# Which PSUM banks the layernorms of a selective-scan stage use, in a kernel that overlaps the scan with the layers behind it

## Chip, cores, metric

The kernel runs on one core of a Trainium2 chip. The metric is device time in microseconds of one execution; lower is better. Times are medians of a few runs.

## What is computed

Input is x, 4 batches of 384 channels by 32 x 32 positions, all float32. Two layers, each a mixer and a feed-forward with residuals:

```
x = x + SS2D(ln_c(x))          # layer 0 mixer: 4-direction selective scan, layernorm, gelu
t = t + MoE(ln_t(t))           # layer 0 FFN: 4 experts, top 2, 384 -> 1536 -> 384
x = x + attention(ln_c(x))     # layer 1 mixer: 8 heads of 64, one weight for q, k and v
t = t + kron_mlp(ln_t(t))      # layer 1 FFN with Kronecker-factored weights

# the recurrence inside SS2D, for each direction k, channel d and state n, along 1024 positions
h = h * exp(dt * A) + dt * u * B
y = sum over n of h * C   (+ D * u)
ln(v) = (v - mean(v)) / sqrt(var(v) + eps)    # over the 384 channels
```

## The kernel before, in words

**The scan part** (`scan_layer`) walks over 32 units: 4 batches, 4 directions, 2 halves of 512 positions. Units 0 to 7 are batch 0, 8 to 15 batch 1, and so on. A unit has three chunks of 128 channels, a chunk four groups g of states (`chunk`, from line 388). Per chunk and group GpSimd multiplies dt*u by B (L419, two instructions of 128x1024), ScalarE makes exp(dt*A) into PSUM (L428), VectorE runs the recurrence (L433), VectorE and GpSimd multiply by C (L440, L447), and TensorE sums over the states into one PSUM bank `acc` with a selection matrix (L454). VectorE then adds `acc` into y (L281, L285). So a unit has 24 instructions of L419, and counting them tells where the scan stands. While a unit is scanned, `project` prepares the next one: matmuls for B, C and dt (L317, L344), the softplus on ScalarE (L348 to L361; for batches 1 to 3 GpSimd helps with L374 and L375), and stores to DRAM from which the scan's operands are read back broadcast by SyncE's DMA queue (L329, L403).

**The layernorms of the scan part** (`layernorm`, L155): over one half of 512 positions a ones-matrix matmul of three channel chunks gives the mean in one PSUM bank (L162), VectorE subtracts it (L164), ScalarE squares (L171), three more matmuls give the variance in a second bank (L175), ScalarE makes the inverse root (L148, L149), VectorE multiplies (L178). It is called for each batch's input (`start`: both halves, when the first unit of that batch is about to be prepared) and for each batch's output (`finish`: once for each half, after the last direction), 16 halves in all. `finish` continues with a GELU (L226), the residual add on GpSimd (L233) and the store to `x1`.

**The tail** (`tail_batch`) is everything after the scan for a batch: `route` (token transposes L635, router, placing of tokens by an indirect DMA L662), `experts` (11 slots: 8 of 256 rows and 3 of 128, each with its expert's two weight matrices fetched by SyncE: matmuls L906 and L921, transposes L889), `combine` (indirect gathers L951, matmuls L958), `prologue`, `attention` (L1007, scores L1030, weights times values L1076, division L1052) and `last_layers` (L1123, L1161, L1178, L1192). It is called from `between(b)`, which after batch b's scan calls the tail of batch b-1. The tail of batch 3 is called after the scan, with other pools.

**PSUM.** There are eight banks of 128 x 512 float32. In the scan part two hold `da` (pool `s_da`), two (pool `s_ps`, tag "ps") are shared by `acc`, the projections `xd_ps` and `dt_ps`, and the layernorms' `mean` and `var`; one (tag "o") and three (tag "p") belong to the `Room` of the tail. Nearly every matmul group of the tail takes a bank of tag "p" by `room.bank("p", ...)`.

**What sets the order.** A scheduler orders each engine's instructions when the program is built. It goes by priorities that follow the order in the source, with an estimate of durations, fills gaps with later work that is ready, and gives out the buffers of a pool by tag. Parts of the tail are marked with `high_priority(offset=FORWARD)`. What it has put in an engine's queue is then fixed. Source order at a batch's end is: `finish` of both halves of batch b, then `tail_batch(b-1)`, then the units of batch b+1.

Of the kernel before, what the change touches and what calls it, by code (L numbers as in the profile page):

```python
# [9 lines left out]
F32 = mybir.dt.float32  # L10
# [7 lines left out]
P = 128  # L18
# [5 lines left out]
HF = 512  # L24
NH = L // HF
# [87 lines left out]
class Body:  # L113
# [38 lines left out]
        at = COL[name][0] + i  # L152
        return self.cols[:, at : at + 1]

    def layernorm(self, src, dst, eps, psum, work, parts=range(NH)):  # L155

        nc = self.nc
        for i in parts:
            sl = halves(i)
            mean = psum.tile([P, HF], F32, tag="ps", name="ln_mean")  # L160
            for c in range(DC):
                nc.tensor.matmul(mean, self.ones, src[:, c, sl], start=(c == 0), stop=(c == DC - 1))  # L162
            for c in range(DC):
                nc.vector.scalar_tensor_tensor(  # L164
                    dst[:, c, sl], mean, -1.0 / D, src[:, c, sl], op0=ALU.mult, op1=ALU.add
                )

            sqs = []
            for c in range(DC):
                sq = work.tile([P, HF], F32, tag="k2", name="ln_sq", bufs=6)  # L170
                nc.scalar.activation(sq, dst[:, c, sl], AF.Square)  # L171
                sqs.append(sq)
            var = psum.tile([P, HF], F32, tag="ps", name="ln_var")
            for c in range(DC):
                nc.tensor.matmul(var, self.ones, sqs[c], start=(c == 0), stop=(c == DC - 1))  # L175
            self.inverse_root(var, var, eps, scale=1.0 / D)
            for c in range(DC):
                nc.vector.tensor_mul(dst[:, c, sl], dst[:, c, sl], var)  # L178

    def scan_layer(self, x1, between):

        nc, tc, a = self.nc, self.tc, self.a
        with ExitStack() as ctx:
            wp = ctx.enter_context(tc.tile_pool(name="s_w", bufs=1))
            work = ctx.enter_context(tc.tile_pool(name="s_work", bufs=1))
            dram = ctx.enter_context(tc.tile_pool(name="s_dram", bufs=3, space=DRAM))
            dap = ctx.enter_context(tc.tile_pool(name="s_da", bufs=2, space=PSUM))
            psum = ctx.enter_context(tc.tile_pool(name="s_ps", bufs=2, space=PSUM))  # L190

            wx = wp.tile([P, DC, KG, XD], F32, tag="wx", name="wx")
            nc.scalar.dma_start(out=wx, in_=a["wx"].rearrange("(c p) k m -> p c k m", p=P))
            nega = wp.tile([P, KG * NB * NG], F32, tag="nega", name="nega")
            lo, hi = COL["alog"]
            nc.scalar.activation(nega, self.cols[:, lo:hi], AF.Exp)
            nc.vector.tensor_scalar_mul(nega, nega, -1.0)
            dsum = wp.tile([P, DC], F32, tag="dsum", name="dsum")
            lo, hi = COL["ds"]
            nc.vector.tensor_reduce(  # L200
                dsum, self.cols[:, lo:hi].rearrange("p (k c) -> p c k", k=KG), AX.X, ALU.add
            )

            sel = wp.tile([P, DB], F32, tag="sel", name="sel")
            nc.vector.tensor_reduce(
                sel, self.ident.rearrange("p (n d) -> p d n", d=DB), AX.X, ALU.add
            )

            def start(b):
                x = work.tile([P, DC, L], F32, tag="u", name="u")  # L210
                src = a["x"][b].rearrange("(c p) l -> p c l", p=P)
                if b > 0:
                    nc.sync.dma_start(out=x, in_=src)
                    self.layernorm(x, x, self.eps6, psum, work)
                    return x

                for i in range(NH):
                    nc.sync.dma_start(out=x[:, :, halves(i)], in_=src[:, :, halves(i)])
                self.layernorm(x, x, self.eps6, psum, work, parts=[0])
                return x  # L220

            def finish(b, y, i):

                self.layernorm(y, y, self.eps5, psum, work, parts=[i])
                for c in range(DC):
                    ins = nc.scalar.activation(  # L226
                        y[:, c, halves(i)], y[:, c, halves(i)], AF.Gelu,
                        bias=self.col("lnb", c), scale=self.col("lnw", c),
                    ).ins
                    rows = slice(c * P, (c + 1) * P)  # L230
                    x = work.tile([P, HF], F32, tag="k2", name="x", bufs=6)
                    nc.sync.dma_start(out=x, in_=a["x"][b][rows, halves(i)])
                    nc.gpsimd.tensor_add(x, x, y[:, c, halves(i)])  # L233
                    nc.sync.dma_start(out=x1[b][rows, halves(i)], in_=x)
                self.exp_again(ins)

            units = [
                (b, k, i)  # L240
                for b in range(B)
                for k in ORDER
                for i in (range(NH) if k < 2 else reversed(range(NH)))
            ]
            us = {0: start(0)}
            ahead = []
            self.place_behind = None
            for _ in self.project(units[0], us[0], wx, work, dram, psum, ahead):
                pass
            self.layernorm(us[0], us[0], self.eps6, psum, work, parts=range(1, NH))  # L250
            self.under_way = {}
            carry = None
            for n, unit in enumerate(units):
                b, k, i = unit
                fed, ahead = ahead, []
                project = iter(())
                if n + 1 < len(units):
                    nb = units[n + 1][0]
                    if nb not in us:
                        us[nb] = start(nb)  # L260
                    project = self.project(units[n + 1], us[nb], wx, work, dram, psum, ahead)
                    next(project)
                if n % NH == 0:
                    carry = wp.tile([P, NB * NG], F32, tag=f"carry{n // NH % 2}", name="carry")
                if k == 0 and i == 0:
                    y = work.tile([P, DC, L], F32, tag="y", name="y")
                for c in range(DC):
                    acc = psum.tile([P, HF], F32, tag="ps", name="acc")
                    for _ in self.chunk(
                        unit, n % NH == 0, c, fed, carry, nega, sel, acc, work, dap  # L270
                    ):
                        next(project, None)
                    if k % 2 == 0:
                        ys = y[:, c, halves(i)]
                        out = acc
                    else:
                        w = slice(i * (HW // NH), (i + 1) * (HW // NH))
                        ys = y[:, c, :].rearrange("p (h w) -> p h w", h=HW)[:, :, w]
                        out = acc.rearrange("p (w h) -> p h w", h=HW)
                    if k == 0:  # L280
                        nc.vector.scalar_tensor_tensor(  # L281
                            ys, us[b][:, c, halves(i)], dsum[:, c : c + 1], out, op0=ALU.mult, op1=ALU.add
                        )
                    else:
                        nc.vector.tensor_add(ys, ys, out)  # L285
                if k == ORDER[-1]:
                    self.under_way.setdefault(b, fed[2])
                    finish(b, y, i)
                    if n + 1 == len(units) or units[n + 1][0] != b:
                        between(b)  # L290
# [1036 lines left out]
def build(nc, a):  # L1327
    with tile.TileContext(nc, schedule_with_timeline_sim=True) as tc, ExitStack() as ctx:
        body = Body(ctx, tc, a)
        dram = ctx.enter_context(tc.tile_pool(name="x1", bufs=1, space=DRAM))  # L1330
        x1 = [dram.tile([D, L], F32, tag=f"x1_{b}", name=f"x1_{b}") for b in range(B)]
        with ExitStack() as tail:
            room = body.open_tail(tail)

            def between(b):
                if b > 0:
                    body.tail_batch(b - 1, x1, room)

            with ExitStack() as banks:
                room.open_banks(banks, NARROW_BANKS)  # L1340
                body.scan_layer(x1, between)
                wide = Room(tc, tail, "w", WIDE)
                wide.open_banks(banks, NARROW_BANKS)
                body.route(B - 1, x1, wide)
                xc = body.first_layer(B - 1, wide)
            with ExitStack() as banks:
                wide.open_banks(banks, WIDE_BANKS)
                body.second_layer(B - 1, xc, wide, lambda: None)
                flag = body.overflow(wide)
# [79 lines left out]
```

## Time and profile before

| | |
|---|---|
| time, median of 3 runs | 4389.3 us (4378.26 to 4389.32) |
| the profiled execution, its own time | 4365.25 us |
| its span, first to last instruction | 4363.5 us |
| PE busy | 3382.3 us, 78% |
| POOL busy | 3049.6 us, 70% |
| DVE busy | 2919.3 us, 67% |
| ACT busy | 2504.0 us, 57% |
| mean granted TensorE clock | 0.86 |
| DMA moved | 684.74 MB, mean 157 GB/s |

Engines: PE is TensorE (PEld its weight loads), DVE VectorE, ACT ScalarE, POOL GpSimd, SP SyncE. In lines by 40 slices each digit is the busy share of one slice (109 us) in tenths. In lines of stretches the columns are start:end, length, then busy time (and instructions) of PE, PEld, DVE, ACT and POOL, the granted TensorE clock, DMA share and GB/s. A line of a group has: source line, engine, operation, written<-read tiles, shapes, count | busy us, mean ns | idle before it and what ended it. The trace counts each float32 matmul of this kernel as two.

### The profile page before, as it was taken

What the parts mean: (1) busy time and instruction counts of PE and PEld (TensorE: products, weight loads), DVE (VectorE), ACT (ScalarE), POOL (GpSimd) and SP (SyncE); (2) the same over time, 40 slices, a digit from 0 to 9 for tenths busy, and PEclk for the clock granted to TensorE, in tenths of its full rate; (3) what the DMA queues carried; (4) which work ended last, traced back from release to release, by engine and by line L of the source; (5) the groups of instructions that cost most, each with busy time, mean ns of one, the idle gap of its engine ahead of it and who ended that gap; (6) DMA issues with size and microseconds to landing.
All of it is one profiled execution on the core that took longest, in us unless ns stands there. A gap on an engine that the chain in (4) does not pass through costs nothing. (4 is left out here: it accounts for less than half of the span.)

```text
span 4363.5 us, 46084 instructions
## 1 busy us (share of the span) xinstructions
PE 3382.3 (78%) x13436; PEld 1581.3 (36%) x13436; DVE 2919.3 (67%) x4331; ACT 2504.0 (57%) x4470; POOL 3049.6 (70%) x1475
## 2 busy tenths in 40 slices
PE   6545544379997895579997888579998799999896
PEld 2111111145553221235554322135554234666323
DVE  5888888967877868968787867968887740200102
ACT  4445545556665875466575777466666564343353
POOL 5999998898988968688898978789898831000100
PEclk7766776589997997779998999679999899999997
DMA  5444354577886534457779534457789434336200
GB/s 136 114 122 116 106 162 115 151 228 214 231 241 183 142 109 139 125 174 213 213 229 279 154 95 132 115 158 225 215 233 273 134 108 142 116 126 214 63 17 15
DMA packets 404756, 684.74 MB, mean 157 GB/s; under 512 B 50960, under 2 KB 206480, under 8 KB 404496
## 3 DMA queue, kind: packets, MB, share of 16 engines
q1 hardware_dynamic: 395184, 655.37, 51.9%
q0 software_dynamic: 8192, 25.17, 1.7%
q8 instruction: 108, 1.77, 0.2%
q14 instruction: 152, 1.25, 0.1%
q10 hardware_dynamic: 1120, 1.18, 0.1%
HBM read 561.47 MB, written 120.06 MB: 156 GB/s over the span
## 5 line engine op out<-in xcount | busy, mean ns | idle before, releaser
L419 POOL TENSOR_TENSOR bx<-dtr,bcs 128x1024 f32<-128x1024 f32 x768 | 1792.4, 2361 | 229.6 <-PE acc L454 118.7
L428 ACT ACTIVATE da<-dtr,nega 128x512 f32<-128x512 f32 x1536 | 1045.3, 690 | 945.8 <-DVE bx L440 564.3
L447 POOL TENSOR_TENSOR bx<-bx,bcs 128x1024 f32<-128x1024 f32 x384 | 903.1, 2359 | 179.1 <-DVE carry L444 74.3
L906 PE MATMUL h_ps<-xc,w 128*128 128x256 f32 (+1 forms) x3168 | 675.0, 368 | 60.8 <-DMA w<-in_w 18.7
L454 PE MATMUL acc<-bx,sel 128*32 128x512 f32 x3072 | 496.8, 697 | 289.2 <-POOL bx L447 232.4
L921 PE MATMUL y_ps<-w,hs 128*128 128x384 f32 x1824 | 643.2, 505 | 38.1 <-ACT hs L914 37.8
L906 PEld LDWEIGHTS h_ps<-xc,w 128*128 128x128 f32 x3168 | 556.1, 200 | 238.7 <-issue 112.8
L433 DVE TENSOR_TENSOR_SCAN bx<-da,carry,bx 128x512 f32<-128x512 f32 x384 | 474.7, 1270 | 129.3 <-ACT da L428 65.8
L433 DVE TENSOR_TENSOR_SCAN bx<-da,bx 128x512 f32<-128x512 f32 x384 | 453.3, 1210 | 117.1 <-POOL bx L419 59.2
L433 DVE TENSOR_TENSOR_SCAN da<-da,carry,bx 128x512 f32<-128x512 f32 x384 | 478.0, 1274 | 66.5 <-ACT da L428 60.9
L440 DVE TENSOR_TENSOR bx<-da,bcs 128x512 f32<-128x512 f32 x768 | 510.3, 680 | 3.7
L433 DVE TENSOR_TENSOR_SCAN da<-da,bx 128x512 f32<-128x512 f32 x384 | 456.2, 1219 | 63.3 <-ACT da L428 53.0
L921 PEld LDWEIGHTS y_ps<-w,hs 128*128 128x128 f32 x1824 | 350.0, 196 | 325.8 <-issue 78.2
L1036 ACT ACTIVATE ex<-s_ps 128x512 f32<-128x512 f32 x512 | 300.8, 592 | 156.6 <-PE s_ps L1030 154.4
L1030 PE MATMUL s_ps<-w 64*128 64x512 f32 x1024 | 307.9, 662 | 53.1 <-ACT ex L1036 51.8
L911 ACT ACTIVATE hs<-h_ps,bb 128x256 f32<-128x256 f32 (+1 forms) x528 | 201.0, 441 | 218.8 <-PE h_ps L906 218.4
L1076 PE MATMUL o_acc<-ex,vt 128*64 128x512 f32 x1024 | 287.0, 638 | 18.1 <-ACT ex L1036 11.5
L454 PEld LDWEIGHTS acc<-bx,sel 128*32 128x32 f32 x3072 | 80.0, 116 | 585.9 <-POOL bx L447 319.8
L942 POOL TENSOR_TENSOR diag<-ident,g_weight 128x1024 f32<-128x1024 f32 x8 | 15.0, 1893 | 345.6 <-PE xc_ps L889 331.0
L925 DVE TENSOR_TENSOR y<-y_ps,bb 128x384 f32<-128x384 f32 x76 | 41.7, 549 | 273.4 <-PE y_ps L921 273.4
L344 PE MATMUL dt_ps<-xd,wdt 12*128 12x512 f32 x192 | 123.2, 726 | 71.4 <-ACT mag L383 43.8
L1030 PEld LDWEIGHTS s_ps<-w 64*128 64x128 f32 x1024 | 82.8, 190 | 256.0 <-ACT ex L1036 206.0
(214 smaller groups left out, 3767.2 us busy)
## 6 DMA issues: line engine op xcount, KB each, us to landing
w<-in_w SPq DMA_DIRECT2D x352, 576.0 KB
dtr<-dd SPq DMA_DIRECT2D x1536, 128.0 KB
bcs<-rows SPq DMA_DIRECT2D x512, 128.0 KB
dd<-one_e SPq DMA_DIRECT2D x96, 256.0 KB
dd<-mag SPq DMA_DIRECT2D x96, 256.0 KB
rows<-zero SPq DMA_DIRECT2D x76, 192.0 KB
xs<-rows SPq DMA_DIRECT2D x32, 384.0 KB
made<-y SPq DMA_DIRECT2D x32, 384.0 KB
```

What stands on the lines that cost most here:

```text
L419: pool = nc.gpsimd.tensor_mul(bx, dtr[q][1], bc[:, 0].unsqueeze(1).to_broadcast([P, 2, HF])).ins
L428: nc.scalar.activation(da, dtr[q][0][:, j, :], AF.Exp, scale=nega[:, col : col + 1])
L433: nc.vector.tensor_tensor_scan(run(h), run(da), run(bx[:, j, :]), 0.0 if first else hold, ALU.mult, ALU.add,)
L440: dve = nc.vector.tensor_mul(bx[:, j, :], h, cg).ins
L447: pool = nc.gpsimd.tensor_mul(bx, bx, cg.unsqueeze(1).to_broadcast([P, 2, HF])).ins
L454: nc.tensor.matmul(acc[lo : lo + DB, :], sel, out[q][:, j, :], start=(g == 0), stop=(g == NG - 1),)
L906: nc.tensor.matmul(ps[:, r, :], w1[(f + r) // wf][:, c, (f + r) % wf * P : ((f + r) % wf + 1) * P], xc[:, c, :], start=(c == 0), stop=(c = ...
L911: nc.scalar.activation(hs[:, f + r, :], ps[:, r, :], AF.Identity, bias=bb[:, f + r : f + r + 1])
L921: nc.tensor.matmul(out[:, :D], hs[:, f, t * P : (t + 1) * P], w2[f // wf][:, f % wf, :], start=(f == 0), stop=(f == FC - 1),)
L1030: ins = nc.tensor.matmul(ps, w[rows, j * P : (j + 1) * P], w[rows, halves(i)], start=True, stop=True).ins
L1036: done.append(nc.scalar.activation(ex[:, o, :], ps, AF.Exp, scale=HD**-0.5, accum_out=sums[:, t, 2 * j + o, i : i + 1],).ins)
L1076: ins = nc.tensor.matmul(out[cols, :], made[t][1][:, j, cols], ex[:, o, :], start=(j == 0), stop=(j == MB - 1),).ins
```

## The change

The layernorms of the scan part take their two banks (`ln_mean`, `ln_var`) from the tail's room, tag "p" (three banks), in place of the scan's own pool (tag "ps", two banks). The pools keep their sizes; the scan's two banks are now shared by `acc`, `xd_ps` and `dt_ps` alone. The `room` is handed through to `scan_layer`.

```
-    def layernorm(self, src, dst, eps, psum, work, parts=range(NH)):
+    def layernorm(self, src, dst, eps, room, work, parts=range(NH)):
...
-            mean = psum.tile([P, HF], F32, tag="ps", name="ln_mean")
+            mean = room.bank("p", "ln_mean")
...
-            var = psum.tile([P, HF], F32, tag="ps", name="ln_var")
+            var = room.bank("p", "ln_var")
...
-    def scan_layer(self, x1, between):
+    def scan_layer(self, x1, room, between):
...
-                    self.layernorm(x, x, self.eps6, psum, work)
+                    self.layernorm(x, x, self.eps6, room, work)
...
-                self.layernorm(x, x, self.eps6, psum, work, parts=[0])
+                self.layernorm(x, x, self.eps6, room, work, parts=[0])
...
-                self.layernorm(y, y, self.eps5, psum, work, parts=[i])
+                self.layernorm(y, y, self.eps5, room, work, parts=[i])
...
-            self.layernorm(us[0], us[0], self.eps6, psum, work, parts=range(1, NH))
+            self.layernorm(us[0], us[0], self.eps6, room, work, parts=range(1, NH))
...
-                body.scan_layer(x1, between)
+                body.scan_layer(x1, room, between)
```

## The prediction, made before the change was run

> **What bounds the kernel now.** I read the share table and the 40 slices first, then busy time by stage, then single groups.
>
> ```profile
> PE 3382.3 (78%) x13436; PEld 1581.3 (36%) x13436; DVE 2919.3 (67%) x4331; ACT 2504.0 (57%) x4470; POOL 3049.6 (70%) x1475
> ...
> PE   6545544379997895579997888579998799999896
> ...
> POOL 5999998898988968688898978789898831000100
> ```
>
> POOL is full while the scan runs (slices 2 to 32), and PE is only half used up to about slice 7, where the feed-forward and attention work (the "tail") begins. One scan unit is 24 multiplications of L419 on POOL, so counting them gives the time at which each unit starts: 43.8 us unit 0, 663.0 unit 7, 774.2 unit 8, 1672.7 unit 16, 2609.0 unit 24, and 3514.5 for the scan's end. The stages, as "window length, PE, PEld, DVE, ACT, POOL busy, PE clock":
>
> ```profile
> 43.80:663.00 619.20, 331.40 (x940) 82.76 (x940) 546.77 (x745) 316.81 (x498) 583.27 (x253) 0.70 0.47 125
> 663.00:774.20 111.20, 51.63 (x164) 15.98 (x164) 90.41 (x110) 61.81 (x96) 92.06 (x45) 0.64 0.44 116
> 899.00:1347.00 448.00, 416.92 (x1753) 249.71 (x1753) 357.56 (x484) 288.73 (x460) 386.42 (x178) 0.95 0.79 226
> 1406.00:1663.00 257.00, 226.42 (x958) 62.39 (x956) 200.37 (x268) 200.33 (x458) 220.91 (x102) 0.97 0.45 126
> 1668.00:1919.00 251.00, 136.48 (x529) 57.21 (x529) 202.05 (x346) 132.45 (x197) 191.08 (x99) 0.71 0.44 133
> 3620.00:4049.00 429.00, 412.83 (x1763) 270.82 (x1759) 44.84 (x94) 165.36 (x278) 10.46 (x3) 0.98 0.42 139
> 3842.00:4049.00 207.00, 191.84 (x846) 137.50 (x844) 11.56 (x21) 78.85 (x118) 3.79 (x2) 0.95 0.51 173
> ```
>
> Row 1 is units 0 to 6, scan alone: 88.5 us a unit, POOL busy 83.3 of them. Row 3 is the experts of batch 0, run during units 8.8 to 13: PE is busy 417 of 448, POOL 386. That stage is held by PE. Row 4 is batch 0's attention, row 5 the next batch's routing with batch 0's last layers: a latency chain in which no engine is full. Rows 6 and 7 lie after the scan: batch 3's experts with most of batch 2's attention, and within them a stretch of almost pure expert work.
>
> In the experts' stretch PE's time divides so:
>
> ```profile
> L906 PE MATMUL h_ps<-xc,w 128*128 128x256 f32 (+1 forms) x792 | 173.3, 375 | 21.6 <-DMA w<-in_w 10.7 <-DVE xc L893 10.7 <-issue 0.2
> L921 PE MATMUL y_ps<-w,hs 128*128 128x384 f32 x456 | 160.2, 502 | 7.8 <-ACT hs L914 7.5 <-DVE carry L444 0.2
> L454 PE MATMUL acc<-bx,sel 128*32 128x512 f32 x400 | 52.1, 604 | 0.0
> ```
>
> The experts' own PE work is 173.3 + 160.2 + 8 of transposes = 341 us a batch. The scan's is 52.1 + 24.4 (L317) + 13.4 (L344) = 90 over 4.25 units: 21 us a unit.
>
> **What the skill says.** "PSUM — Partial Sum Buffer", section "Engine vs sequencer instructions": MATMULs start and complete in program order, and the queues of ScalarE, VectorE and GpSimd are strict FIFO. The trace agrees: in the stretch of row 5 PE idled 22.0 us for L454 behind POOL's L447 (16.9 at the longest), with tail matmuls queued. So the static order decides who waits. "Perfetto Trace Analysis", section "Optimization Strategy": a kernel with several regimes can gain from interleaving them. Rows 1 and 3 are two such regimes, and before does interleave them. "TensorE: Matmul & The Clock Gate", Part 1: PE's clock is throttled by default and activity releases it. The trace agrees (0.70 in row 1, 0.95 in row 3). I take expert durations from the busy rows.
>
> **The change part by part.** No instruction is added or removed: each of 16 layernorm halves still issues 3 + 3 matmuls and takes two banks, from the tag of three ("p") that every tail matmul group shares, not from the scan's tag of two. Direct price: three banks in place of two can only spare the layernorm's chain, which costs some 15 us at a batch boundary (row 2: 111.2 against 88.5, part of it routing). A gain of 0 to 10 us at each of three boundaries; I count it as zero.
>
> What matters is the queue for "p". In the built programs I place tail work by how many scan units' L454 matmuls stand ahead of it on PE:
>
> ```
>                            before             after
> batch 0 routing (L635)     7.0 and 8.25       16.08 to 16.25
> batch 0 experts (L906)     8.8 to 12.9        16.75 to 18.75
> batch 0 attention (L1076)  13.4 to 15.8       19.4 to 22.0
> batch 0 last (L1192)       17.25 to 17.6      23.0
> batch 1 experts            17.7 to 21.8       24.1 to 26.3
> batch 1 last               25.75 to 26.1      30.5 to 30.9
> batch 2 experts            26.3 to 30.4       after the scan
> ```
>
> In after batch 0's routing stands behind batch 1's last layernorm: banks of "p" go out in the order of allocation in the source, where finish(1) precedes tail_batch(0). Even the small wg_ps, at the start of PE in before, moves behind unit 16. So (a) units 8 to 15 run without a tail, (b) two tails are packed into units 16 to 31, each in about 7 units in place of 9 to 10, and (c) the third lies bare behind the scan. The other queues move with it: POOL's indirect DMAs (L662, L951) from units 8.8 and 13.3 to 16.75 and 19.3, and SP's weight loads with the experts.
>
> *(a)* From batch 1 on, POOL also has six 1.27 us subtractions (L374, L375) a unit: 7.6 + 88.5 = 96 us alone. Unit 16 then starts at 43.8 + 619.2 + 103 (unit 7: 88.5 + 15) + 105 (unit 8, with the second finish) + 6 x 96 + 110 (unit 15, with layernorms) = 1557, where before has 1672.7: a gain of 116.
>
> *(b)* In after the tail holds its places in PE's queue, and the scan's matmuls between them are few. The stretch lasts as long as the longer of tail and scan.
> - Start and routing: 8 + 90 (before: first late tt_ps at 817, experts at 899).
> - Experts, with 2.35 units: alone they take 357 (row 7: 207 us for 5.5 slots of 256 rows, so 37.6 a slot; a batch has 9.5), and 2.35 x 21 of scan matmuls: 406. POOL alone would need 226, so the scan is held up by 180.
> - Combine: 58 (before: 1347 to 1406).
> - Attention, 2.67 units: POOL needs 256, row 4 took 257 for 2.5. Value 267, bounds 250 and 280.
> - Routing and last layers, 1 unit: row 5's chain is 251; batch 1's ran 2703 to 2912, 209. Value 200, bounds 180 and 225.
>
> Sum: 1557 + 8 + 90 + 406 + 58 + 267 + 200 = 2586 at unit 23; with unit 23 and its layernorms (115) unit 24 starts at 2701 (before 2609).
> - Batch 1: 15 + experts with 2.5 units 357 + 53 = 410, + 58 + attention 270 + routing and last 205 = 958, then 1.08 units, 112. The scan ends at 3771 (before 3514.5).
>
> *(c)* After the scan, before has 849 us. After has: batch 2's experts 357 + 25 for the last layernorm and routing = 382; batch 3's experts with batch 2's whole attention 357 + 157 (PE busy in the bare attention, 4093 to 4253) = 514; batch 2's last layers with batch 3's combine 115; batch 3's attention 160; last layers 110.5. Sum 1281.
>
> Span 3771 + 1281 = 5052. Before's profiled execution has span 4363.5 and time 4365.25, so 5054 on its scale. The median shown, 4389.3, lies 24 above that execution; I add it: 5078, rounded to 5080, or 16% slower.
>
> The cover: what hid batch 2's experts was units 26 to 30 of the scan; without it they cost their full 357. Where the scan's waits for banks go, PE order is late next.
>
> **Rivals.**
> 1. *Packed tails cost the scan no more than before's did.* Units 16 to 31 keep before's 936.3 + 905.5: 1557 + 1842 + 1281 = 4680, by median 4705. For: total PE work is the same. Against: experts at 2.35 units need 406 us of PE, and POOL has work for 226.
> 2. *Faster: the tail's place in PE's queue doesn't bind the scan.* If POOL sets the pace everywhere, units 16 to 31 take 16 x 96 + 40 = 1576, and a perfectly packed end takes PE's 2 x (341 + 157 + 60) = 1116: 4249, by median 4275. It decides where the scan stays under 95 us a unit through 16 to 31 (4363.5 - 1557 - 1281 = 1525), or the end shrinks below 1230. Against: before had 117 and 113 a unit there with tails less dense.
> 3. *Slower still: the packed order makes PE wait for the scan too.* If each packed tail takes its upper bounds (100 + 440 + 62 + 280 + 225 = 1107, 86 over the 1021 above) and the end 80 more: 5052 + 2 x 86 + 80 = 5304, by median 5330.
> 4. *The order doesn't change.* Excluded by the built programs.
>
> **Numbers.** Forecast 82%, rival 1 10%, rival 2 2%, rival 3 6%. Own bounds: the packed tails 75 either way each, together 150, the end 70, stretch (a) 20, which gives 4840 to 5320; I extend a little towards rival 1: 4800 to 5310. About 0.3% either way is what a measurement can tell from no change: faster 2%, same 1%, slower 97%.
>
> **What would show it.** Unit 16 starting near 1557 with no tail matmul on PE before it; an experts stretch of about 406 us over some 2.4 units, PE over 90% busy and POOL near 55%; the scan's end near 3770; some 1280 us with POOL idle after it. The forecast is wrong if POOL stays at 85% or more through units 16 to 19, or if less than 1150 us follow the scan.

## The result: 11% slower

The changed kernel takes 4870.5 us (median of 5, 4862.8 to 4876.4) against 4386.9 us of before: a ratio of 1.1105, 95% interval 1.1088 to 1.1122. The forecast was 5080, range 4800 to 5310. The profiled execution took 4862.8 us with a span of 4861.0. The page of after, engines by 40 slices (of 122 us now):

```profile
PE   6455553333344699788566998886569999999796
...
POOL 5999989999999654899749557998851010002000
```

Slices 7 to 13 show what is new: POOL full, PE at three or four tenths, so a scan alone. Then, twice, PE goes to 9 while POOL falls to 4 or 5 (slices 15 and 16, 23 and 24), and the end with POOL nearly empty takes ten slices of 122 us, where before had seven of 109. The start of units by counting L419, as in the prediction:

| | unit 16 | unit 24 | scan's end | end |
|---|---|---|---|---|
| before | 1672.7 | 2609.0 | 3514.5 | 4363.5 |
| after | 1518.9 | 2614.7 | 3586.7 | 4861.0 |
| stretch, after less before | -153.8 | +159.5 | +66.5 | +425.3 |

The sum is the whole difference of the spans, 497.5 us. (The medians differ by 483.6, because the profiled execution of before lay 22 us under its median and that of after 8.) The stages of after, columns as in the prediction: units 0 to 6; units 8 to 15; batch 0's experts; its attention; the next routing with batch 0's last layers; behind the scan batch 2's experts, then batch 3's experts with batch 2's attention.

```profile
46.10:652.80 606.70, 323.96 (x927) 79.53 (x926) 542.45 (x738) 315.93 (x497) 580.59 (x251) 0.69 0.48 127
764.00:1518.90 754.90, 283.19 (x912) 50.42 (x912) 648.47 (x866) 380.63 (x590) 731.50 (x344) 0.58 0.44 118
1637.00:2001.00 364.00, 356.87 (x1545) 235.18 (x1545) 205.33 (x283) 201.75 (x322) 211.32 (x98) 0.99 0.75 223
2063.00:2311.00 248.00, 216.70 (x966) 57.55 (x967) 207.37 (x270) 195.36 (x454) 235.91 (x108) 0.99 0.46 121
2311.00:2520.00 209.00, 116.04 (x447) 51.86 (x444) 139.93 (x287) 98.24 (x144) 123.78 (x65) 0.68 0.46 138
3586.60:3963.00 376.40, 342.29 (x1419) 251.65 (x1420) 46.42 (x141) 124.92 (x201) 27.64 (x24) 0.94 0.60 193
3963.00:4463.00 500.00, 492.18 (x2013) 276.73 (x2013) 36.24 (x76) 205.41 (x457) 26.60 (x20) 1.00 0.41 132
```

In row 3 PE is busy 98% of the stretch and POOL 58%. Before, the same expert matmuls took 448 us with POOL busy 86%: more of the scan was done beside them. What POOL waits for in that stretch, after and then before (899 to 1347 us):

```profile
L419 POOL TENSOR_TENSOR bx<-dtr,bcs 128x1024 f32<-128x1024 f32 x56 | 130.6, 2364 | 128.0 <-PE acc L454 126.8 <-DMA bcs<-rows 1.2
L419 POOL TENSOR_TENSOR bx<-dtr,bcs 128x1024 f32<-128x1024 f32 x102 | 238.4, 2362 | 27.2 <-DMA dtr<-dd 12.0 <-PE acc L454 11.7 <-issue 3.3
```

After has 56 multiplications (2.3 units) and 126.8 us of waiting for L454, the scan's own matmuls, which read `bx` last and stand in PE's queue among the experts'. Before, the same wait was 11.7 us over 102 multiplications. PE's order binds, which the second rival denied.

One thing in this trace was not in the prediction. From 2440 to 2542 us no matmul of L454 runs. POOL in order of time (start, length, idle before it):

```profile
2480.06 2.35 POOL L447 TENSOR_TENSOR bx<-bx,bcs 128x1024 f32<-128x1024 f32 x1 [3.86 <-DVE bx L433]
2533.41 3.72 POOL L233 TENSOR_TENSOR x<-x,y 128x512 f32<-128x512 f32 x3 [51.01 <-ACT y L226]
2543.34 13.90 POOL L419 TENSOR_TENSOR bx<-dtr,bcs 128x1024 f32<-128x1024 f32 x6 [6.21 <-PE acc L454]
```

and PE at the end of batch 0's last layers:

```profile
2507.81 3.63 PE L1178 MATMUL f_acc<-hs,wc 128*32 128x512 f32 x12 [5.23 <-ACT hs L1170]
...
2519.69 2.74 PE L162 MATMUL ln_mean<-y,ones 128*128 128x512 f32 x6
```

Batch 2's output layernorm begins at 2519.7, when batch 0's last layers have left the banks (their fo_ps matmuls end at 2520). Behind it follow its GELU (L226), then the residual add on POOL (L233), and behind that in POOL's queue the scan's L419. PE's queue is held too: the scan's L454 stands behind the layernorms there and then runs 24 records in a row from 2542.2. So the queue for banks holds up the scan as well as the tail; e1 below is the test of it.

### The profile page after: what moved, and what is told of

It is laid out like the page before. It is cut to its first block, busy times and chain, and to the rows that moved or that the text cites. A ratio compares the mean times of both kernels' runs of the same rounds, so it can differ in the third digit from the quotient of the medians.

```text
span 4861.0 us, 46200 instructions
## 1 busy us (share of the span) xinstructions
PE 3447.6 (71%) x13436; PEld 1577.2 (32%) x13436; DVE 2895.3 (60%) x4331; ACT 2517.6 (52%) x4468; POOL 3045.4 (63%) x1475
## 5 line engine op out<-in xcount | busy, mean ns | idle before, releaser
L419 POOL TENSOR_TENSOR bx<-dtr,bcs 128x1024 f32<-128x1024 f32 x768 | 1794.5, 2370 | 375.1 <-PE acc L454 317.1
L454 PE MATMUL acc<-bx,sel 128*32 128x512 f32 x3072 | 591.9, 814 | 722.3 <-POOL bx L447 643.6
L906 PE MATMUL h_ps<-xc,w 128*128 128x256 f32 (+1 forms) x3168 | 637.4, 357 | 22.7 <-DMA w<-in_w 18.3
L921 PE MATMUL y_ps<-w,hs 128*128 128x384 f32 x1824 | 616.7, 492 | 16.2 <-ACT hs L914 14.3
L906 PEld LDWEIGHTS h_ps<-xc,w 128*128 128x128 f32 x3168 | 540.1, 193 | 157.6 <-issue 63.7
L454 PEld LDWEIGHTS acc<-bx,sel 128*32 128x32 f32 x3072 | 85.6, 125 | 1144.9 <-POOL bx L447 850.2
L1117 POOL TENSOR_TENSOR xt<-xt,wb 128x3072 f32<-128x3072 f32 x4 | 26.8, 6689 | 644.1 <-DMA wb<-in_wb 644.1
L344 PE MATMUL dt_ps<-xd,wdt 12*128 12x512 f32 x192 | 135.4, 792 | 155.9 <-ACT mag L383 108.5
L893 DVE COPY xc<-xc_ps 128x512 f32<-128x512 f32 (+2 forms) x76 | 41.0, 555 | 310.8 <-PE xc_ps L889 295.9
```

The costliest lines, as they stand in the source:

```text
L419: pool = nc.gpsimd.tensor_mul(bx, dtr[q][1], bc[:, 0].unsqueeze(1).to_broadcast([P, 2, HF])).ins
L454: nc.tensor.matmul(acc[lo : lo + DB, :], sel, out[q][:, j, :], start=(g == 0), stop=(g == NG - 1),)
L906: nc.tensor.matmul(ps[:, r, :], w1[(f + r) // wf][:, c, (f + r) % wf * P : ((f + r) % wf + 1) * P], xc[:, c, :], start=(c == 0), stop=(c = ...
L921: nc.tensor.matmul(out[:, :D], hs[:, f, t * P : (t + 1) * P], w2[f // wf][:, f % wf, :], start=(f == 0), stop=(f == FC - 1),)
```

## The experiments

The theory was *order*: banks of one tag go out in the order of the source, so a late layernorm keeps the earlier batch's tail off its banks, and the place of the tail makes the time. The main rival was *banks*: layernorm and tail get in each other's way because they share three. All ratios are to the kernel before, run on the same chip in the same series; its median was 4384.7 for e1 to e4, 4361.8 for e5 to e8, 4363.8 for e9 to e11, 4363.6 for e12.

### The delay alone, banks as before (e1)

```
+            self.depend(ins, self.last_ln)      # wg_ps in moe_consts
...
+                        if s == 0:
+                            self.depend(ins, self.last_ln)      # first xc_ps of each batch's experts
```

`last_ln` is the last variance matmul of the layernorms written so far; `depend` makes its first instruction wait for its second.

> The kernel before with its banks as they were (layernorms in the scan's own two), and only three kinds of dependency added: the first matmul on the router weights and the first transposes of each batch's experts wait for the last variance matmul of the layernorms that stand ahead of that tail in the source. In the built order the tail then stands where the changed kernel has it (batch 0's routing at unit 16.2, its experts at 16.8 to 19.3, batch 2's experts after the scan). Theory, order: the delay alone makes the time, 4850 to 4920 us. Rival, banks: what costs is that layernorms and tail share three banks; here they don't, so about 4390 us.

Measured: 4836.6 us, 1.1037 (1.1018 to 1.1055), just under the low end of what was expected. With every bank where it was, 94% of the loss is there (0.1037 of 0.1105). Unit 16 starts at 1529.1, the experts of batch 2 at 3578 behind the scan, whose end is 3561.3. The banks rival falls. About 0.7% is left over. Units 16 to 23 take 1041.0 us here and 1095.8 in the changed kernel, and 41 of these 55 us lie in units 22 and 23; units 0 to 15 and 24 to 31 give part of it back. POOL's waits between 2400 and 2640 us, here:

```profile
POOL bx L449 <- DVE bx L435: 13.9, 5, 5.1
...
POOL x L235 <- ACT y L228: 7.9, 2, 4.6
```

and in the changed kernel and in before:

```profile
POOL x L233 <- ACT y L226: 51.0, 1, 51.0
POOL x L233 <- ACT y L226: 8.7, 1, 8.7
```

The residual add waits 7.9 or 8.7 us where the layernorm has the scan's banks, 51.0 where it queues for the tail's.

### Sharing banks without the delay (e2)

```
-                    self.layernorm(x, x, self.eps6, room, work)
+                    self.layernorm(x, x, self.eps6, shared if b < 2 else own, work)
...
-                self.layernorm(y, y, self.eps5, room, work, parts=[i])
+                self.layernorm(y, y, self.eps5, shared if b < 1 else own, work, parts=[i])
```

`shared` takes tag "p" of the room, `own` tag "ps" of the scan.

> The changed kernel, but only the 6 of 16 layernorm halves that precede the first tail in any case (inputs of batches 0 and 1, output of batch 0) take the tail's banks; the other 10 take the scan's own. Theory, order: no tail is held up by more than a unit, so the time is that of before within 1.5%: 4320 to 4450 us. Rival, banks: a share of the loss in proportion to the halves, 6/16 of 484 us: about 4570 us.

Measured: 4313.9 us, 0.9832 (0.9815 to 0.9849): faster than both kernels. The expected range holds it, but a gain was not expected. Units 3 to 6 take 83 to 84 us each, where before has 86.5 to 88.8, and the scan ends at 3487.2 in place of 3514.5; 849 us behind the scan become 832. What makes e2 faster than before was not separated.

### A bank of their own, and what one tail bank is worth (e3, e4)

```
-NARROW_BANKS = {"o": 1, "p": 3}
+NARROW_BANKS = {"o": 1, "p": 2, "l": 1}      # e3, with room.bank("l", ...) in layernorm
+NARROW_BANKS = {"o": 1, "p": 2}              # e4, on the kernel before
```

> The changed kernel with a bank of their own for the layernorms (tag l, one bank), taken from the tail, which keeps two. No layernorm stands in the tail's queue for banks, and none in the scan's. Theory, order: the tail stands nearly where it stood before (experts of batch 0 at units 8.8 to 13, batch 2's end just after the scan), so 4380 to 4500 us, most of what is above before being the tail's lost bank, and within 1% of the next kernel. Rival, banks: the layernorms use fewer banks than in the changed kernel and the tail loses one, so at least 4600 us.

> The kernel before with two banks for the tail in place of three, layernorms in the scan's two: the price of one bank of the tail by itself. Theory, order: batch 2's experts still stand before the scan's end (27.3 to beyond 31), 4400 to 4520 us. Rival, banks: the tail lives by its third bank, 4600 us or more.

Measured: e3 4422.8 us, 1.0088 (1.0071 to 1.0104); e4 4455.0 us, 1.016 (1.0143 to 1.0176). Losing one of three banks costs the tail 1.6%. On top of that, layernorms in a bank of their own gain 0.7%. The changed kernel gives the tail more banks than e3 and is 10% slower: the number of banks is not what it lacks.

### The source in the order of time (e5, e6)

```
+            def ahead(b):
+                if b > 0:
+                    with tc.high_priority(offset=-12000):
+                        body.early(b - 1, x1, room)      # routing of batch 0, experts, attention
...
-                    body.tail_batch(b - 1, x1, room)
+                    body.late(b - 1, x1, room)           # routing of b, last layers of b-1
```

`ahead(b)` is called in `scan_layer` before the first unit of batch b. What it writes gets a lowered priority, so that it still fills gaps only. e5 makes this move in the changed kernel, e6 in the kernel before.

> The changed kernel with all 16 layernorm halves still in the tail's three banks; only the place of the tail in the source moves. Routing, experts and attention of batch b-1 are written ahead of batch b's units, and so ahead of that batch's layernorms in the queue for banks (with a lowered priority, so that they still only fill gaps); routing of b and the last layers of b-1 stay behind finish(b). In the built order the experts then stand at units 8.9 to 13, 17.8 to 22 and 25.8 to 30. Theory, order: the loss goes without any change of banks, 4280 to 4420 us. Rival, banks: layernorms and tail still share three banks, so it stays above 4600 us.

> The same move of the source on the kernel before (layernorms in the scan's own two banks). Built order as before within a tenth of a unit. Theory: 4360 to 4410 us, as before; the move in the source does nothing where no bank queue stands between. If it gains or loses over 1%, part of what the kernel e5 shows is the move itself and not the queue for banks.

Measured: e5 4471.1 us, 1.0243 (1.0223 to 1.0263); e6 4370.6 us, 1.0021 (1.001 to 1.0033). With all 16 halves still in the tail's banks, 78% of the loss goes (0.0862 of 0.1105) by moving the tail in the source; in the kernel before the same move does next to nothing (e6). e5 missed its range by 51 us all the same: units 15 and 23 take 183 and 250 us, in e6 133 and 127. In this order the layernorms at a batch's end stand behind the attention in the queue for banks.

### The tail as gap filler (e7)

```
-                    body.tail_batch(b - 1, x1, room)
+                    with tc.high_priority(offset=-FORWARD):
+                        body.tail_batch(b - 1, x1, room)
```

> The changed kernel with the whole tail at a priority below the scan's, as gap filler. In the built order batch 0's experts are spread over units 16.7 to 20.8 in place of 16.7 to 19, but batch 0's last layers still end before the layernorms of unit 23, and batch 1's end behind the scan. Theory, order: between unit 16 and 23 the tail's own chain sets the time, so spreading it gains nothing and what falls behind the scan is added: 4900 to 5100 us. Rival, density: the loss in units 16 to 31 comes from packing the tail denser than the scan can bear, and goes when the scan has priority: about 4700 us.

Measured: 4770.8 us, 1.0936 (1.0914 to 1.0957). Neither expectation holds: it is faster than the changed kernel, by 1.5% as the ratios go, not slower, and still above the rival's 4700. By spans, units 16 to 23 take 1068.5 us (changed kernel 1095.8). The scan runs ahead and then stops: unit 23 alone takes 294 us. POOL's waits between 2280 and 2600 us:

```profile
POOL rows L662 <- DVE g_weight L833: 76.4, 1, 76.4
POOL x L233 <- ACT y L226: 68.3, 1, 68.3
```

It waits for the next batch's routing (L662) and for the residual add (L233), so there the tail's chain sets the time, as I had said. Units 24 to 31 take 838.8 in place of 971.9, and the part behind the scan 1343.4 in place of 1274.3. I had added batch 1's last layers behind the scan in full (200 us); what came back was 69. Net, the span is 90 us shorter (the ratios give 74), so of the 226 us that units 16 to 31 had lost some 75 to 90 are the price of the tail's precedence over the scan.

### Half of the layernorms each (e8, e9)

```
-                    self.layernorm(x, x, self.eps6, shared if b < 2 else own, work)      # as in e2
+                    self.layernorm(x, x, self.eps6, shared, work)      # e8, outputs own
+                    self.layernorm(x, x, self.eps6, own, work)         # e9, outputs shared
```

> The changed kernel with only the input layernorms (8 of 16 halves) in the tail's banks, the output ones in the scan's. The input layernorms of batch 2 stand about one unit earlier than the output ones of batch 1, so the tail starts at unit 15.0 in place of 16.1 and batch 2's experts at 30.5 in place of behind the scan. Theory, order, by the measured stages of the changed kernel: one unit less of bare scan (about 110 us), some 45 us less at unit 23 and 54 at unit 31, 35 us given back: 4640 to 4760 us. Rival, a share by halves: half of the loss, 4630 us or less.

> The changed kernel with only the output layernorms (8 of 16 halves) in the tail's banks, the input ones in the scan's. In the built order the tail stands as in the changed kernel (batch 0's routing at 16.1, batch 2's experts behind the scan). What it takes away is the other side of the queue: in the changed kernel the input layernorms of batch 3 start when batch 0's last layers have left their banks, and the scan's sums pause from 2440 to 2542 us. Theory, order with a wait on both sides: the late tail stays and the pause shrinks, as in e1, so 4800 to 4850 us. Rival: the pause at unit 23 comes from something else (the tail's chain, or the output layernorms), 4855 to 4885 us. Rival, halves: half of the loss, 4630 us.

Measured: e8 4679.1 us, 1.0732 (1.0708 to 1.0755), within the range that the stages gave: the tail one unit earlier, with the output layernorms out of its banks, is worth 3.4%. The two were not separated. Most of it (147 of 192 us of span) is gained behind the scan, 65 in units 16 to 23. e9 4864.6 us, 1.1151 (1.1128 to 1.1174): as slow as the changed kernel, so my theory of the pause fell and its rival, the output layernorms, holds. In e9 batch 0's two input halves stay in the tail's banks too, so it shares 10 of 16 halves, not 8. I had put the pause on the input layernorms. Here batch 3's first input mean runs early, the second half's as late as ever:

```profile
2430.93 5.13 PE L162 MATMUL ln_mean<-u,ones 128*128 128x512 f32 x6 [7.52 <-DMA u<-in_x]
2528.61 2.74 PE L162 MATMUL ln_mean<-u,ones 128*128 128x512 f32 x6
```

So e9 frees the inputs only in part. But what POOL stands at is the output's residual add (2400 to 2640 us):

```profile
POOL x L239 <- ACT y L232: 52.8, 1, 52.8
```

In e8, with the outputs in the scan's banks, that wait is 4.1 us (2300 to 2580 us), and unit 23 takes 124 us in place of 201, though there the tail also stands a unit earlier.

### Which half dries the scan out in e5 (e10, e12)

e10 is e5 with the output layernorms (and batch 0's input) in the tail's banks, e12 with the input ones alone.

> Kernel e5 (tail moved in the source) with only the output layernorms in the tail's banks, the input ones in the scan's. Kernel e5 lost 50 us at unit 15 and 120 us at unit 23. Theory: there the input layernorms wait for the attention to leave the three banks and the scan runs dry; with them in the scan's banks 4330 to 4420 us. Rival: the pauses come from GpSimd's queue, where the residual add of the output layernorm waits behind the GELU and the last layers' bias add for its weights; then it stays at 4440 to 4480 us.

> Kernel e5 (tail moved in the source) with only the input layernorms in the tail's banks, the output ones in the scan's: the counterpart of e10. In the built order the attention's scores end ahead of unit 15's end as in e5 and e10. Theory after e9 and e10: it is the output layernorm, held behind the tail's banks, whose GELU and residual add then block GpSimd's queue; with it in the scan's banks the pauses at units 15 and 23 go, 4310 to 4370 us. Rival: either half is enough, since input layernorms that wait for the attention's last bank leave the scan without its next operands; then 4420 to 4480 us.

Measured: e10 4475.6 us, 1.0257 (1.023 to 1.0283); e12 4432.2 us, 1.0161 (1.0138 to 1.0184). Freeing the inputs gains nothing. Freeing the outputs gains 0.8%, not the 2% or more that I expected: unit 15 still takes 189 us and unit 23 236. POOL's waits around unit 23 (2500 to 2780 us in e5, 2490 to 2760 in e12), e5:

```profile
POOL xt L1132 <- DMA wb<-in_wb: 93.9, 1, 93.9
POOL x L233 <- ACT y L226: 39.1, 1, 39.1
```

e12:

```profile
POOL xt L1138 <- DMA wb<-in_wb: 77.0, 1, 77.0
POOL bx L427 <- PE acc L462: 49.2, 3, 40.4
```

The wait for the residual add is gone in e12 and one for the scan's matmuls stands in its place; the last layers' bias add (`xt`, L1117 in the kernel before) blocks POOL for 77 to 98 us there in e5, e10 and e12, and in e6 not at all while the scan runs. So either half is enough to make pauses. e6 differs from e5 in the layernorms' banks alone, so the sharing brings the bias add's wait with it; by what path, no run shows.

### The router's constants first (e11)

```
+                body.moe_consts(room)
                 body.scan_layer(x1, room, between)      # on e2
```

> Kernel e2 (6 of 16 halves in the tail's banks, 4314 us) with the router's constants prepared ahead of the scan, so that their matmul no longer stands behind the layernorms of unit 7 (it stood at unit 8.0, now at 0; experts at 8.9 as before). Theory: a matmul group of 1 us that is not the last thing that the routing waits for, so no difference to e2 beyond 0.5%: 4295 to 4335 us. Rival: the router constants hold up batch 0's routing by their place; then a gain of 1% or more, 4270 us or less.

Measured: 4317.2 us, 0.989 (0.9871 to 0.9909). No gain over e2, as the ratio goes rather 0.6% less. The small matmul group that moved so far in the built order holds nothing up. e2 stays the fastest version.

## Why the prediction was right, step by step

- **The queue for "p" delays the tail by a batch: right, and shown.** The delay alone (e1) makes 94% of the loss, sharing without delay (e2) none, and undoing the order with the same banks (e5) takes 78% away. The price was set too high: a rise of 691 us was forecast, 484 was measured. (a), both packed tails and (c) all came out shorter than forecast, so these sums did not cancel, though single terms in them went both ways; the result lies near the low end of the range. Of the signs named ahead, the experts' stretch (364 us over 2.3 units, PE 98% busy, POOL 58%) and the bare end (1274 us) came as said; unit 16 started 38 us earlier, and the scan ended at 3587, not near 3770.
- **(a) bare scan in units 8 to 15: sign right, gain 116 forecast, 154 measured.** The mis-sized term is the unit from batch 1 on, 96 us: units 9 to 14 took 91.4, which makes 27 of the 38. I had carried over the 5.2 us a unit in which POOL stood idle in batch 0 (88.5 less 83.3); in units 9 to 14 POOL was busy 545.3 of 548.6 us, so idle for 0.5 us a unit. Units 0 to 6 gave another 13; the rest nearly cancels.
- **(b) experts hold up the scan: mechanism right, 406 forecast, 364 measured.** The mis-sized term is their own PE work, 341 us: here it is 154.2 + 151.5 + 9.1 = 315. That is 26 of the 42; PE's idle time (7 in place of 16) and the scan's matmuls (42 in place of 49) are the rest. The granted clock was 0.99, not 0.95, which would turn 341 into some 327 (an estimate: 341 x 0.95 / 0.99). The first matmul group took 352 ns a piece in place of 375, more than the clock's share; why was not tried. I had taken durations from a busy stretch; a fuller one was faster still. The sum's 2.35 units were not the 2.0 of its own table (16.75 to 18.75); 2.33 were measured.

The groups of PE in batch 0's experts:

```profile
L906 PE MATMUL h_ps<-xc,w 128*128 128x256 f32 (+1 forms) x792 | 154.2, 352 | 0.8 <-DVE xc L893 0.8
L921 PE MATMUL y_ps<-w,hs 128*128 128x384 f32 x456 | 151.5, 489 | 0.0
L454 PE MATMUL acc<-bx,sel 128*32 128x512 f32 x216 | 30.1, 619 | 0.0
```

- **The rest of (b):** routing 118 (98 forecast), combine 62 (58), attention 248 (267), routing and last layers 209 (200), unit 23 after them 95 (115): 1096 with the experts, where I had 1144. Batch 1's stretch: 972 against 1070, again with the experts' 385 against 425, and 74 against 112 for what is left of the scan.
- **(c) the bare third tail: right.** 376, 500, 125, 160 and 113 us, 1274 in all, where the sum had 382, 514, 115, 160 and 110.5, 1281.
- The span came out at 4861 where I had 5052: 38 from (a), 48 and 98 from the two packed tails, 7 from (c) make the 191. The median lies another 18 lower: I had added 24 for the distance of before's median from its profiled execution, and after's lay only 8 above.
- **"A gain of 0 to 10 us at each of three boundaries", counted as zero: looked for in the wrong place.** Unit 7, with the first boundary, takes 111.2 us in both kernels (in before with part of the routing beside it), but units 0 to 6 take 606.7 in place of 619.2. Wherever batch 0's input layernorms are out of the scan's pool (after, e2, e3, e5, e7 to e12) units 3 to 6 take 83 to 85 us; where they are in it (before, e1, e4, e6) 86 to 89. In the first group PE runs the scan's sums in smaller pieces between the softplus matmuls of the next unit; why the pool changes that order was not tried.
- **Missed:** that the queue works both ways. Output layernorms wait for the tail, and through GELU and residual add they stop POOL. It cost some 40 us in units 22 and 23 (by e1) and lay within the range.
- **Rival 1** (packed tails cost no more than before's did, 4705) fell: units 16 to 31 took 2068 us, not 1842. But the forecast had 2214 there, and the measured time lies nearer to this rival (165 above) than to the forecast (210 below). e7 shows that some 75 to 90 of those 226 us were priority, not work.
- **Rivals 2 and 3** fell too: the scan took 129 us a unit through units 16 to 31, not under 95, and the packed tails took 1096 and 972 us, less than the forecast's 1144 and 1070, not more.

## What to carry over

Before letting two streams share a tag of buffers, look where their allocations stand in the source: the pool serves them in that order, and the stream that comes later in time but earlier in the text holds up the other by as much as lies between them. Price such a change from the built order: count how much of the stage that bounds the kernel (here units of the scan) lies beside each piece of the other stream, and then price each stretch by the engine that holds it. A share that hardly moves the tail (e2) went with a gain of 1.7%; the same share for all batches cost 11%.

## What the runs showed that I had not expected

PE's clock in the trace followed how densely it was fed: 0.58 in the bare scan of units 8 to 15 (PE busy 38% of the time), 0.95 in before's experts (93%), 0.98 to 0.99 in the experts packed into the scan (96 to 98%). This agrees with the Trainium skill, "TensorE: Matmul & The Clock Gate", Part 1, that activity releases the clock. So the denser packing of a stage that PE holds went with less PE time for the same experts (341 to 315 us, of which the clock accounts for some 14 by the estimate above), while it stretched the scan beside it.
